# Last stage of a four-layer convolution block: raw results are added a part later from two buffers of their own, and the loads of strips, h2 and the boxes' x2 are issued a step ahead

## The chip, the cores and the metric

One NeuronCore of a Trainium2 chip runs the whole kernel. The time is that of the device, in microseconds (us); before the change the median of three runs is 4706.14 us (4699.86, 4706.14 and 4724.04).

The engines in this text: PE is TensorE (matrix products and transposes), DVE is VectorE, ACT is ScalarE, POOL is GpSimd. SP (SyncE) only issues transfers here; its instruction queue is called SPq. Each engine works through its own list in order, and waits at an instruction until what that instruction needs has been signalled.

## What is computed

An image tensor x of 4 x 384 x 64 x 64 in float32 goes through four layers, each `x = x + layer(group_norm(x))`. The change lies in the fourth alone, a 7x7 convolution, one filter for each channel and batch, whose filter depends on the input:

```python
x_avg = x.mean(axis=(2, 3)); x_max = x.max(axis=(2, 3))
x_w = gelu(x_avg @ w_avg.T + b_avg + x_max @ w_max.T + b_max)
xr  = (x_w[:, :, None] * w_mix[None]).reshape(b, c, 7, 7)
Gx  = sqrt(sum(xr * xr, axis=(2, 3)))            # keepdims
Nx  = Gx / (Gx.mean(axis=1) + EPS)
kern = gamma * (xr * Nx) + beta
out = depthwise_conv(x, kern, padding=3)
```

Here `x` is the normalised input, and `out` is added to the un-normalised one. For a channel and batch, `kern` is a factor times `w_mix` plus a constant `beta`. So the result is a sum of three things: the input itself (x2 below); `a_s` times the convolution with `w_mix`, which doesn't depend on the batch (the "raw" result); and `b_s` times the sum over a 7x7 window (the "boxes").

## The kernel before

There are B = 4 batches and NJ = 3 groups j of P = 128 channels; a tile is one (j, b): 128 channels on the partitions, N = 4096 pixels, 2 MB. The last stage is `phase_g`. It works in float32, and these are its parts.

*Strips.* The convolution wants pixels on the partitions. `to_strips` (L2094) makes them for j = 0 from x2 in SBUF at the beginning. `half_strips` makes them for a later j in two halves of 64 channels, each in six pieces: load a piece of x2 from memory (L2034, tag `y`, two buffers), scale it (L2040, ACT, tile `ax`), transpose it (L2044, PE, `strip_m`), and copy it out of PSUM into `z` (L2049 on DVE, L2051 on ACT).

*Convolution.* `conv7(j, c0)` handles a chunk of 8 channels. Of the chunk's weights `wmix` (L2132, loaded by POOL, four buffers, asked for three chunks ahead) DVE or POOL makes band matrices `toep` (L2151), four a chunk; PE multiplies (L2164, `conv_m`; the profile shows two records for each float32 product, so 64 for a chunk). For j < 2 ACT copies the result to `rest_o` (L2174), and ACT's queue stores it to memory as `raw` (L2179). For j = 2 `rest_o` has been loaded (L2143) with what the boxes have left, DVE adds the convolution (L2176), and SP stores the end result (L2181).

*x2 of the seven tiles not made earlier.* `x2_of`: load `wx` (L2068), and in four quarters load `h2` (L2073, tile `g_h`, tag `w7`, three buffers), scale it into PSUM (L2077, ACT, `x_m`), add (L2078, DVE), take sums of squares and the maximum (L1868, ACT, which writes over `g_h`), store x2 (L2082, POOL). Then `factors` computes `a_s` and `b_s`, which need all batches.

*Boxes.* `boxes(j, b)` loads x2 again (L2059, tile `in_x`, three buffers of 2 MB shared with the x2 tiles). In four parts of 16 rows it sums over rows on POOL (L2223, L2225) and DVE (L2227 to L2242), transposes (L2248, PE, `ht_m`), copies (L2250, ACT, `ht`), sums over columns with a banded matrix (L2273, PE, `box_m`), and adds `b_s` times that into `in_x` (L2275, DVE). A part makes two such pieces, so 12 tiles make 96. For j < 2 a part also loads the raw result (L2203, SPq, tile `in_raw`, 0.5 MB), scales it by `a_s` (L2258, ACT) and adds it (L2259, DVE): 32 parts, called p = 0 to 31 below. A finished tile is stored by POOL, to `out` for j < 2 (L2263) and to `rest` for j = 2 (L2265). The order of tiles is j = 2, 0, 1.

Four buffers of 0.5 MB with the tag `rest` serve `rest_o`, `in_raw` and, at the start, two of `to_strips`' pieces in turn.

*Order.* Everything beside the convolution is written as generators, and the loop in `phase_g` draws on them: a piece of strips at the first step of a chunk; steps of x2 while there are any; after that a step of boxes at each of a chunk's five steps, and two at the first step of every second chunk. The source's order isn't the machine's: the framework's scheduler places each instruction in its engine's list by a clock of its own, as soon as it takes operands and buffers to be free there, so the position in the source is a priority, not a place.

Of the kernel before, what the change touches and what calls it, by code (L numbers as in the profile page):

```python
# [13 lines left out]

# [7 lines left out]
F32 = mybir.dt.float32  # L22
AF = mybir.ActivationFunctionType
# [4 lines left out]
N = H * W  # L28
NJ = 3
P = 128  # L30
# [251 lines left out]
class _Builder:  # L282
# [1592 lines left out]
    def phase_g(self):  # L1875
# [8 lines left out]
        with ExitStack() as ctx:  # L1884
# [34 lines left out]

            x2 = [self.x2_of(j, b) for j, b in ((1, 1), (1, 2), (1, 3), (2, 0), (2, 1), (2, 2), (2, 3))]  # L1920
            x2 = self.in_turn(*x2, self.factors())
            boxes = self.in_turn(*(self.boxes(j, b) for j in (2, 0) for b in range(B)))
            boxes1 = self.in_turn(*(self.boxes(1, b) for b in range(B)))
            self.mix_ahead = []
            for n in range(3):
                self.load_mix(n)
            x2_left = True
            for j in range(NJ):
                for half in range(2):
                    strips = self.half_strips(j + half, 1 - half) if 0 < j + half < NJ else iter(())  # L1930
                    for n in range(8):
                        for k, _ in enumerate(self.conv7(j, 64 * half + 8 * n)):
                            if k == 0:
                                next(strips, None)
                            if not x2_left:
                                for _ in range(2 if k == 0 and n % 2 else 1):
                                    next(boxes, None)
                            elif k == 0 or k == 1 and n % 4 < 3:
                                x2_left = next(x2, "none") != "none"
                    for _ in strips:  # L1940
                        pass
                if j == 1:
                    boxes = self.in_turn(boxes, boxes1)
            for _ in boxes:
# [69 lines left out]
    def pair_scales(self, j):  # L2014

        for half in range(2):
            for u in range(2):
                for k, v in enumerate((self.s_s, self.s_b)):
# [3 lines left out]
                    )  # L2022

    def half_strips(self, j, half):

        nc = self.nc
        for pair in range(2):
            for part in range(3):
                y = self.gt_p.tile([P, 11 * P], F32, tag="y", name="ax2", bufs=2)
                lo, hi = (22 * part - 1) * W, (22 * part + 21) * W  # L2030
                inside = slice(max(lo, 0) - lo, min(hi, N) - lo)
                for u in range(2):
                    src = self.scratch["x2"][2 * pair + u][j][64 * half : 64 * half + 64]
                    nc.sync.dma_start(y[64 * u : 64 * u + 64, inside], src[:, max(lo, 0) : min(hi, N)])  # L2034
                if part == 0:
                    nc.gpsimd.memset(y[:, 0:W], 0.0)
                if part == 2:
                    nc.gpsimd.memset(y[:, N - lo :], 0.0)
                s, b = (self.a_pair[:, j, k, half, pair : pair + 1] for k in range(2))
                nc.scalar.activation(y[:, inside], y[:, inside], AF.Identity, bias=b, scale=s)  # L2040
                for i, (k0, n) in enumerate(((0, 4), (4, 4), (8, 3))):
                    m = self.pm("strip_m")
                    for k in range(n):
                        nc.tensor.transpose(m[:, k * P : (k + 1) * P], y[:, (k0 + k) * P : (k0 + k + 1) * P], self.ident)  # L2044
                    mv = m.rearrange("p (k b c) -> p k b c", b=2, c=64)[:, 0:n]
                    at = 1 + 11 * part + k0
                    zv = self.z[:, 64 * half : 64 * half + 64, at : at + n, 2 * pair : 2 * pair + 2]
                    if i == 1:
                        nc.vector.tensor_copy(zv.rearrange("p c k b -> p k b c"), mv)  # L2049
                    else:  # L2050
                        nc.scalar.copy(zv, mv.rearrange("p k b c -> p c k b"))  # L2051
                yield

# [7 lines left out]

    def x2_of(self, j, b):

        nc = self.nc
        at = lambda v: v[:, j, b : b + 1]
        bias = at(self.g0) if j == NJ - 1 else self.zero
        x = self.gx_tile("x2")
        nc.sync.dma_start(x, self.wx[b][:, j])  # L2068
        for q in range(4):
            sl = slice(q * 1024, (q + 1) * 1024)  # L2070

            h = self.gw_p.tile([P, 1024], F32, tag="w7", name="g_h2", bufs=3)
            nc.sync.dma_start(h, self.h2[b][:, j, sl])  # L2073
            for v in range(2):
                m = self.pm("x2_m")
                part = slice(q * 1024 + v * 512, q * 1024 + v * 512 + 512)
                nc.scalar.activation(m, h[:, v * 512 : v * 512 + 512], AF.Identity, bias=bias, scale=at(self.gh))  # L2077
                nc.vector.tensor_add(x[:, part], x[:, part], m)  # L2078

            self.x2_piece(j, b, q, x[:, sl], h)  # L2080
            yield None
        nc.gpsimd.dma_start(self.scratch["x2"][b][j], x)  # L2082
        yield x

    def to_strips(self, j, b, x, first=False):
# [49 lines left out]
    def conv7(self, j, c0):  # L2135
# [47 lines left out]

    def boxes(self, j, b):

        nc = self.nc
        x = self.load_x2(j, b)
        off = lambda k: self.off[:, j, b, k - 6 : k - 5]  # L2190
        pairs_of = lambda t, r, n: t[:, r * W : (r + 2 * n) * W].rearrange("p (k r w) -> p k r w", r=2, w=W)
        above, last = None, None
        for part in range(4):
            r0 = 16 * part
            edge = above
            if part < 3:

                above = self.gt_p.tile([P, 2, W], F32, tag="edge", name="edge", bufs=2)
                nc.gpsimd.tensor_copy(above, pairs_of(x, r0 + 12, 2)[:, :, 1])

            if j < NJ - 1:
                d = self.gt_p.tile([P, 1024], F32, tag="rest", name="in_raw", bufs=4)
                nc.sync.dma_start(  # L2203
# [51 lines left out]
            self.box_sums(j, b, x, 2 * part + 1, ht)  # L2255
            if j < NJ - 1:
                xp = x[:, part * 1024 : (part + 1) * 1024]
                nc.scalar.activation(d, d, AF.Identity, bias=self.g0[:, j, b : b + 1], scale=self.a_s[:, j, b : b + 1])  # L2258
                nc.vector.tensor_add(xp, xp, d)  # L2259
            if part == 3:  # L2260
                if j < NJ - 1:

                    nc.gpsimd.dma_start(self.out[j].rearrange("(b m) c n -> b (m c n)", b=B)[b].rearrange("(c n) -> c n", c=P), x)  # L2263
                else:
                    nc.gpsimd.dma_start(self.rest[:, :, b], x.rearrange("p (y n) -> p y n", n=P))  # L2265

# [41 lines left out]
```

## Time and profile before

| what | value |
|---|---|
| median of three runs | 4706.14 us |
| profiled execution, device time | 4704.82 us |
| its span in the profile | 4703.1 us |
| granted clock of PE, mean | 0.969 of full |
| last stage, from its first load to the end | 4012.6 to 4703.1 us |

Of the span the busy shares are PE 93%, DVE 61%, ACT 42% and POOL 17%. How to read this: PE's share is an average over the four layers, and the last stage is 690 us of it. A busy PE isn't necessarily at its peak, since matrix products overlap and the profile models their ends. An engine's idle time is put down to whatever came last before the waiting instruction, a "releaser"; `<-DMA` is a transfer that had to land.

The instructions of the stage from 4250 us on that the text comes back to, with their mean durations:

| line, engine | what | number | mean ns |
|---|---|---|---|
| L2164 PE | `conv_m` product | 1764 | 282 |
| L2273 PE | `box_m` product | 768 | 293 |
| L2250 ACT | `ht` copy | 96 | 582 |
| L2258 ACT | scaling of `in_raw` | 32 | 1241 |
| L2259 DVE | adding `in_raw` | 32 | 1558 |
| L2275 DVE | adding a box piece | 96 | 745 |
| L2151 DVE | `toep` | 72 | 1211 |
| L2151 POOL | `toep` | 35 | 2434 |
| L2132 POOL | issuing a `wmix` load | 24 | 591 |

An entry like `x8` in the timeline below stands for eight instructions of one kind in a row; the bracket behind it is the time the engine waited before, and for what.

### The profile page before, as it was taken

Reading aid. Unit: us, or ns where it says so; the run is one execution under the profiler, and the core shown is the slowest. Engines: PE = TensorE matmul, PEld = TensorE weight load, DVE = VectorE, ACT = ScalarE, POOL = GpSimd, SP = SyncE. Lnnn points to the kernel's source line nnn. Section 1 sums busy time; section 2 is a strip of 40 time slices with the busy share of each in tenths; the row PEclk is TensorE's granted clock in tenths of the full one; section 3 lists DMA queues with packets and bytes.
Section 4 is the critical chain, followed back from the end, with each engine's and each line's share of the span. In section 5 each row is a group of like instructions: output and inputs, shape, how many; then the busy total and the mean of one; then the engine's idle time right before and its main releaser. Section 6 shows DMA issues by size and latency. Waiting matters only on the chain. (4 is left out here: it accounts for less than half of the span.)

```text
span 4703.1 us, 49799 instructions
## 1 busy us (share of the span) xinstructions
PE 4354.0 (93%) x18445; PEld 2417.9 (51%) x18445; DVE 2851.5 (61%) x4680; ACT 1992.2 (42%) x2937; POOL 801.9 (17%) x760
## 2 busy tenths in 40 slices
PE   7999999999999999998988999699999999788887
PEld 2233444344443444444548888344444444688887
DVE  7766566655566446545877888655531115777788
ACT  4444444444444444444535666311134334663332
POOL 1000000000000000000025566000000000346554
PEclk9999999999999999998989999799999999898999
DMA  4301211121111111112338999766664336795786
GB/s 145 108 33 52 89 66 68 47 75 41 54 67 65 61 34 67 55 53 82 125 105 284 324 336 327 277 259 255 247 241 173 124 131 228 282 331 173 238 282 211
DMA packets 284321, 730.36 MB, mean 155 GB/s; under 512 B 22331, under 2 KB 122790, under 8 KB 272806
## 3 DMA queue, kind: packets, MB, share of 16 engines
q1 hardware_dynamic: 213096, 407.56, 27.1%
q0 software_dynamic: 38880, 173.96, 9.8%
q10 hardware_dynamic: 32094, 145.57, 7.8%
q8 instruction: 149, 2.44, 0.2%
q14 instruction: 102, 0.84, 0.1%
HBM read 433.13 MB, written 293.86 MB: 155 GB/s over the span
## 5 line engine op out<-in xcount | busy, mean ns | idle before, releaser
L822 ACT ACTIVATE probs<-sc_s 128x1024 f32<-128x1024 f32 x512 | 496.7, 1020 | 687.3 <-PE av L932 588.1
L932 PE MATMUL av<-probs,vt 128*128 128x512 f32 x1536 | 714.8, 602 | 0.0
L1137 DVE SCALAR_TENSOR_TENSOR acc<-band,vecs,acc 128x512 f32<-128x512 f32 x708 | 496.1, 745 | 44.8 <-POOL band L1096 39.6
L1424 PE MATMUL conv_m<-toep,z 128*128 128x192 f32 (+1 forms) x2304 | 447.9, 352 | 21.4 <-DVE z L1353 12.0
L932 PEld LDWEIGHTS av<-probs,vt 128*128 128x128 f32 x1536 | 275.6, 191 | 338.1 <-issue 334.3
L1791 PE MATMUL h_m<-f_h,cm_w_t 128*128 128x512 f32 x1008 | 437.6, 597 | 9.8 <-ACT f_h L1728 7.4
L1424 PEld LDWEIGHTS conv_m<-toep,z 128*128 128x128 f32 x2304 | 403.8, 195 | 45.4 <-ACT d_o L1435 15.3
L2164 PE MATMUL conv_m<-toep,z 128*128 128x128 f32 x3072 | 385.3, 283 | 14.9 <-DVE toep L2151 11.7
L2164 PEld LDWEIGHTS conv_m<-toep,z 128*128 128x128 f32 x3072 | 371.7, 199 | 17.0 <-DVE toep L2151 11.3
L1670 PE MATMUL h_s<-e_tok,cm_w_t 128*128 128x512 f32 x768 | 362.6, 594 | 4.1 <-DVE e_tok L1655 4.1
L1791 PEld LDWEIGHTS h_m<-f_h,cm_w_t 128*128 128x128 f32 x1008 | 192.8, 191 | 254.1 <-issue 239.9
L814 PE MATMUL sc_s<-q,k 32*128 32x512 f32 x2048 | 306.9, 643 | 14.6 <-ACT probs L822 14.4
L1405 POOL TENSOR_TENSOR toep<-w,band 128x1280 f32<-128x1280 f32 x96 | 278.2, 2898 | 201.0 <-PE conv_m L1424 189.0
L1058 PE MATMUL t_m<-w_in_t,xb 128*128 128x384 f32 x768 | 278.4, 497 | 4.1 <-DVE coef L1075 4.0
L968 PE MATMUL proj_m<-xm,w_proj_t 128*128 128x512 f32 x576 | 271.9, 611 | 6.0 <-DVE xm L907 4.9
L1677 ACT COPY e_h<-h_s 128x1024 f32<-128x1024 f32 x96 | 97.2, 1013 | 399.4 <-PE h_s L1670 399.4
L1679 DVE BATCH_NORM_STATS2 h_st<-e_h 128x6 f32<-128x512 f32 x192 | 123.5, 685 | 217.3 <-ACT e_h L1677 217.2
L1670 PEld LDWEIGHTS h_s<-e_tok,cm_w_t 128*128 128x128 f32 x768 | 146.3, 191 | 187.9 <-issue 183.2
L975 DVE SCALAR_TENSOR_TENSOR x_res<-proj_m,bn_c,x_res 128x512 f32<-128x512 f32 x96 | 71.7, 747 | 237.3 <-PE proj_m L968 237.1
L1058 PEld LDWEIGHTS t_m<-w_in_t,xb 128*128 128x128 f32 x768 | 142.7, 192 | 141.2 <-issue 59.1
L1670 PE MATMUL h_s<-z,cm_w_t 128*128 128x512 f32 x384 | 196.1, 592 | 0.0
L837 PE MATMUL av<-probs,vt 128*32 128x512 f32 x1536 | 189.0, 604 | 4.4 <-DVE av_t L866 4.4
(464 smaller groups left out, 6333.2 us busy)
## 6 DMA issues: line engine op xcount, KB each, us to landing
d<-d_o ACTq DMA_DIRECT2D x48, 1024.0 KB
c_d<-d SPq DMA_DIRECT2D x48, 1024.0 KB
hid<-e_h ACTq DMA_DIRECT2D x16, 3072.0 KB
f_h<-hid SPq DMA_DIRECT2D x14, 3072.0 KB
x_in<-in_x SPq DMA_DIRECT2D x96, 256.0 KB
x_res<-in_x SPq DMA_DIRECT2D x32, 768.0 KB
xa<-x_res POOLq DMA_DIRECT2D x32, 768.0 KB, 3.7
xa_out<-xa SPq DMA_DIRECT2D x32, 768.0 KB
```

Source lines behind the costliest of these rows:

```text
L814: nc.tensor.matmul(s[:, g], lhsT=k4[32 * g : 32 * g + 32, c], rhs=q[i][32 * g : 32 * g + 32], start=True, stop=True,)
L822: nc.scalar.activation(p[:, h * 1024 : (h + 1) * 1024], s[:, 2 * h : 2 * h + 2].rearrange("p a b -> p (a b)"), AF.Exp, scale=0.25,)
L837: nc.tensor.matmul(av[k][quarter(g)], lhsT=vt[:, 4 * c + v, quarter(s)], rhs=p[:, v * 512 : (v + 1) * 512], start=c == 0 and not before, s ...
L932: nc.tensor.matmul(av[0], lhsT=vt[:, 4 * c + v, :], rhs=p[:, v * 512 : (v + 1) * 512], start=c == 0 and v == 0, stop=c == 7 and v == 3,)
L968: nc.tensor.matmul(m, lhsT=self.w_proj[:, j, o * P : (o + 1) * P], rhs=xm[:, j], start=j == 0, stop=j == NJ - 1,)
L1058: nc.tensor.matmul(m[:, 0:C], lhsT=xb[:, j], rhs=self.w_in[:, j, :], start=j == 0, stop=j == NJ - 1,)
L1137: nc.vector.scalar_tensor_tensor(out, src(j, k), w, done, ALU.mult, ALU.add)
L1405: eng.tensor_tensor(t, self.w53[:, at : at + 160].rearrange("p (m n) -> p m n", n=8).unsqueeze(2).to_broadcast([P, 20, 8, 8]), band.rearra ...
L1424: nc.tensor.matmul(m[:, c * 256 + to : c * 256 + to + 64 * (k1 - k0)], lhsT=self.z_[:, at : at + P], rhs=t[:, 10 * c + k0 : 10 * c + k1].r ...
L1670: nc.tensor.matmul(s[:, v, :], lhsT=w1[:, j, o * P : (o + 1) * P], rhs=t[j][:, v * 512 : (v + 1) * 512], start=j == 0, stop=j == NJ - 1,)
L1791: nc.tensor.matmul(m, lhsT=w2[:, o, j * P : (j + 1) * P], rhs=h[o][:, v * 512 : (v + 1) * 512], start=o == 0, stop=o == 5,)
L2164: nc.tensor.matmul(m[:, ch % 4 * P : (ch % 4 + 1) * P], lhsT=self.z_[:, at : at + P], rhs=t[:, 8 * c + 2 * i : 8 * c + 2 * i + 2].rearrang ...
```

## The change

*Raw results.* `in_raw` gets a tag of its own, `raw`, with two buffers, and the tag `rest` goes from four to three. Scaling and adding move to `after_part`, which is called at the end of the next part (`due`), so the source has them one part after the load; the store of a tile moves with them. In the changed program these are the load L2248, the add L2220, and the stores L2224 and L2226.

*Strips.* `strip_load` loads piece n + 1 before piece n is scaled and transposed, and one step of the generator goes to the first load alone, so that each piece is worked on a chunk later in the source. The tag `y` keeps two buffers.

*h2.* `x2_rest` runs over the quarters of all seven tiles and loads quarter n + 1, and with a tile's first quarter also its `wx`, before quarter n is used. The tag `w7` keeps three buffers.

*The boxes' x2.* `all_boxes` asks for the next tile's x2 in the fourth step of a tile (of twelve), where before it was asked for at the tile's own first step. The three 2 MB buffers stay.

*wmix.* Three buffers in place of four, and a tile is asked for two chunks ahead.

No arithmetic is added or removed. With the function bodies that only move left out:

```diff
@@ phase_g
-            x2 = [self.x2_of(j, b) for j, b in ((1, 1), (1, 2), (1, 3), (2, 0), (2, 1), (2, 2), (2, 3))]
-            x2 = self.in_turn(*x2, self.factors())
-            boxes = self.in_turn(*(self.boxes(j, b) for j in (2, 0) for b in range(B)))
-            boxes1 = self.in_turn(*(self.boxes(1, b) for b in range(B)))
+            x2 = self.x2_rest((1, 1), (1, 2), (1, 3), (2, 0), (2, 1), (2, 2), (2, 3))
+            x2 = self.in_turn(x2, self.factors())
+            boxes = self.all_boxes([(j, b) for j in (2, 0, 1) for b in range(B)])
+            self.ready_raw = [False] * NJ
             self.mix_ahead = []
-            for n in range(3):
+            for n in range(2):
                 self.load_mix(n)
...
-                if j == 1:
-                    boxes = self.in_turn(boxes, boxes1)
+                self.ready_raw[j] = True
...
+    def strip_load(self, j, half, pair, part):
...
+        y = self.gt_p.tile([P, 11 * P], F32, tag="y", name="ax2", bufs=2)
...
+            nc.sync.dma_start(y[64 * u : 64 * u + 64, inside], src[:, max(lo, 0) : min(hi, N)])
...
     def half_strips(self, j, half):
...
+        parts = [(pair, part) for pair in range(2) for part in range(3)]
+        ahead = [self.strip_load(j, half, *parts[0])]
+        yield
+        for n, (pair, part) in enumerate(parts):
+            if n + 1 < len(parts):
+                ahead.append(self.strip_load(j, half, *parts[n + 1]))
+            y, inside = ahead.pop(0)
...
+            yield
...
-    def x2_of(self, j, b):
...
-        x = self.gx_tile("x2")
-        nc.sync.dma_start(x, self.wx[b][:, j])
-        for q in range(4):
-            sl = slice(q * 1024, (q + 1) * 1024)
-
-            h = self.gw_p.tile([P, 1024], F32, tag="w7", name="g_h2", bufs=3)
-            nc.sync.dma_start(h, self.h2[b][:, j, sl])
+    def x2_load(self, j, b, q):
+
+        if q == 0:
+            self.x2_now[j, b] = self.gx_tile("x2")
+            self.nc.sync.dma_start(self.x2_now[j, b], self.wx[b][:, j])
+        h = self.gw_p.tile([P, 1024], F32, tag="w7", name="g_h2", bufs=3)
+        self.nc.sync.dma_start(h, self.h2[b][:, j, q * 1024 : q * 1024 + 1024])
+        return h
+
+    def x2_rest(self, *tiles):
...
+        self.x2_now, parts = {}, [(j, b, q) for j, b in tiles for q in range(4)]
+        ahead = [self.x2_load(*parts[0])]
+        for i, (j, b, q) in enumerate(parts):
+            at = lambda v: v[:, j, b : b + 1]
+            if i + 1 < len(parts):
+                ahead.append(self.x2_load(*parts[i + 1]))
+            h, x = ahead.pop(0), self.x2_now[j, b]
...
@@ to_strips
-            tag, bufs = ("y", 2) if k0 % 16 else ("rest", 4)
+            tag, bufs = ("y", 2) if k0 % 16 else ("rest", 3)
@@ load_mix
-            t = self.gt_p.tile([P, 8 * 64], F32, tag="wmix", name="wmix", bufs=4)
+            t = self.gt_p.tile([P, 8 * 64], F32, tag="wmix", name="wmix", bufs=3)
@@ conv7
-        self.load_mix(16 * j + c0 // 8 + 3)
-        o = self.gt_p.tile([P, 8, P], F32, tag="rest", name="rest_o", bufs=4)
+        self.load_mix(16 * j + c0 // 8 + 2)
+        o = self.gt_p.tile([P, 8, P], F32, tag="rest", name="rest_o", bufs=3)
...
-    def boxes(self, j, b):
...
-        x = self.load_x2(j, b)
+    def all_boxes(self, tiles):
+
+        x, self.due = self.load_x2(*tiles[0]), None
+        for i, (j, b) in enumerate(tiles):
+            ahead = None
+            for n, _ in enumerate(self.boxes(j, b, x)):
+                if n == 3 and i + 1 < len(tiles):
+                    ahead = self.load_x2(*tiles[i + 1])
+                yield
+            x = ahead
+        self.due()
+
+    def after_part(self, j, b, part, x, d):
+
+        nc = self.nc
+        if d is not None:
+            xp = x[:, part * 1024 : (part + 1) * 1024]
+            nc.scalar.activation(d, d, AF.Identity, bias=self.g0[:, j, b : b + 1], scale=self.a_s[:, j, b : b + 1])
+            nc.vector.tensor_add(xp, xp, d)
+        if part == 3:
...
@@ boxes
-                d = self.gt_p.tile([P, 1024], F32, tag="rest", name="in_raw", bufs=4)
+                d = self.gt_p.tile([P, 1024], F32, tag="raw", name="in_raw", bufs=2)
...
             self.box_sums(j, b, x, 2 * part + 1, ht)
-            if j < NJ - 1:
-                xp = x[:, part * 1024 : (part + 1) * 1024]
-                nc.scalar.activation(d, d, AF.Identity, bias=self.g0[:, j, b : b + 1], scale=self.a_s[:, j, b : b + 1])
-                nc.vector.tensor_add(xp, xp, d)
...
+            if self.due:
+                self.due()
+            self.due = partial(self.after_part, j, b, part, x, d)
```

More of the change, by code (lines that the diff above doesn't have):

```diff
@@ L13 @@
 from contextlib import ExitStack, nullcontext
+from functools import partial
 import numpy as np
@@ L2022, in pair_scales @@
                     )
+    def strip_load(self, j, half, pair, part):
+        nc = self.nc
+        y = self.gt_p.tile([P, 11 * P], F32, tag="y", name="ax2", bufs=2)
+        lo, hi = (22 * part - 1) * W, (22 * part + 21) * W
+        inside = slice(max(lo, 0) - lo, min(hi, N) - lo)
+        for u in range(2):
+            src = self.scratch["x2"][2 * pair + u][j][64 * half : 64 * half + 64]
+            nc.sync.dma_start(y[64 * u : 64 * u + 64, inside], src[:, max(lo, 0) : min(hi, N)])
+        if part == 0:
+            nc.gpsimd.memset(y[:, 0:W], 0.0)
+        if part == 2:
+            nc.gpsimd.memset(y[:, N - lo :], 0.0)
+        return y, inside
@@ L2024, in half_strips @@
     def half_strips(self, j, half):
         nc = self.nc
[L2027 to L2052, printed above, removed]
@@ new lines, in half_strips @@
+        parts = [(pair, part) for pair in range(2) for part in range(3)]
[5 more added lines that the diff above has]
+            y, inside = ahead.pop(0)
+            s, b = (self.a_pair[:, j, k, half, pair : pair + 1] for k in range(2))
+            nc.scalar.activation(y[:, inside], y[:, inside], AF.Identity, bias=b, scale=s)
+            for i, (k0, w) in enumerate(((0, 4), (4, 4), (8, 3))):
+                m = self.pm("strip_m")
+                for k in range(w):
+                    nc.tensor.transpose(m[:, k * P : (k + 1) * P], y[:, (k0 + k) * P : (k0 + k + 1) * P], self.ident)
+                mv = m.rearrange("p (k b c) -> p k b c", b=2, c=64)[:, 0:w]
+                at = 1 + 11 * part + k0
+                zv = self.z[:, 64 * half : 64 * half + 64, at : at + w, 2 * pair : 2 * pair + 2]
+                if i == 1:
+                    nc.vector.tensor_copy(zv.rearrange("p c k b -> p k b c"), mv)
+                else:
+                    nc.scalar.copy(zv, mv.rearrange("p k b c -> p c k b"))
+            yield
@@ L2060, in load_x2 @@
         return x
-    def x2_of(self, j, b):
-        nc = self.nc
-        at = lambda v: v[:, j, b : b + 1]
-        bias = at(self.g0) if j == NJ - 1 else self.zero
-        x = self.gx_tile("x2")
-        nc.sync.dma_start(x, self.wx[b][:, j])
-        for q in range(4):
-            sl = slice(q * 1024, (q + 1) * 1024)
-            h = self.gw_p.tile([P, 1024], F32, tag="w7", name="g_h2", bufs=3)
-            nc.sync.dma_start(h, self.h2[b][:, j, sl])
+    def x2_load(self, j, b, q):
[6 more added lines that the diff above has]
+    def x2_rest(self, *tiles):
+        nc = self.nc
+        self.x2_now, parts = {}, [(j, b, q) for j, b in tiles for q in range(4)]
[5 more added lines that the diff above has]
+            h, x = ahead.pop(0), self.x2_now[j, b]
             for v in range(2):
@@ L2076, in x2_of @@
                 part = slice(q * 1024 + v * 512, q * 1024 + v * 512 + 512)
+                bias = at(self.g0) if j == NJ - 1 else self.zero
                 nc.scalar.activation(m, h[:, v * 512 : v * 512 + 512], AF.Identity, bias=bias, scale=at(self.gh))
                 nc.vector.tensor_add(x[:, part], x[:, part], m)
[L2080 to L2083, printed above, removed]
+            self.x2_piece(j, b, q, x[:, q * 1024 : q * 1024 + 1024], h)
+            yield
+            if q == 3:
+                nc.gpsimd.dma_start(self.scratch["x2"][b][j], x)
+                yield
     def to_strips(self, j, b, x, first=False):
@@ L2182, in conv7, with boxes @@
         yield
-    def boxes(self, j, b):
-        nc = self.nc
-        x = self.load_x2(j, b)
+    def all_boxes(self, tiles):
[5 more added lines that the diff above has]
+                    ahead = self.load_x2(*tiles[i + 1])
+                yield
+            x = ahead
+        self.due()
+    def after_part(self, j, b, part, x, d):
+        nc = self.nc
+        if d is not None:
[3 more added lines that the diff above has]
+        if part == 3:
+            if j < NJ - 1:
+                to = self.out[j].rearrange("(b m) c n -> b (m c n)", b=B)[b].rearrange("(c n) -> c n", c=P)
+                nc.gpsimd.dma_start(to, x)
+            else:
+                nc.gpsimd.dma_start(self.rest[:, :, b], x.rearrange("p (y n) -> p y n", n=P))
+    def boxes(self, j, b, x):
+        nc = self.nc
+        assert j == NJ - 1 or self.ready_raw[j]
         off = lambda k: self.off[:, j, b, k - 6 : k - 5]
@@ L2199, in boxes @@
                 nc.gpsimd.tensor_copy(above, pairs_of(x, r0 + 12, 2)[:, :, 1])
+            d = None
             if j < NJ - 1:
-                d = self.gt_p.tile([P, 1024], F32, tag="rest", name="in_raw", bufs=4)
+                d = self.gt_p.tile([P, 1024], F32, tag="raw", name="in_raw", bufs=2)
                 nc.sync.dma_start(
@@ L2255, in boxes @@
             self.box_sums(j, b, x, 2 * part + 1, ht)
-            if j < NJ - 1:
-                xp = x[:, part * 1024 : (part + 1) * 1024]
[L2258 to L2265, printed above, removed]
+            if self.due:
+                self.due()
+            self.due = partial(self.after_part, j, b, part, x, d)
     def box_sums(self, j, b, x, n, ht):
```

## The prediction

> **What bounds the kernel now.** First I read the page's head and its 40 slices: TensorE (PE) busy 93% of 4703.1 us, a fall at slice 34, where the DMA digits rise. The change touches only the last stage, which starts when `mean<-in_consts` is issued at 4012.6 us, so at most 690 us are in question. Next, the stretches of that stage, cut where its own steps change: x2 tiles until 4250, boxes of j=2 until 4412, then boxes of j=0 and 1, beside the convolution of j=2 from about 4430.
>
> ```profile
> core 0: us, PE busy (x) PEld busy (x) DVE busy (x) ACT busy (x) POOL busy (x), PEclk, DMA share, GB/s
> 4050.00:4250.00 200.00, 171.30 (x1431) 168.65 (x1432) 144.12 (x156) 119.76 (x183) 79.90 (x64) 0.93 0.95 328
> 4250.00:4412.00 162.00, 143.80 (x1170) 140.90 (x1169) 118.96 (x166) 56.89 (x93) 109.41 (x111) 0.93 0.59 184
> 4412.00:4560.00 148.00, 121.91 (x997) 119.67 (x996) 115.28 (x149) 53.89 (x74) 85.31 (x78) 0.91 0.85 261
> 4560.00:4694.00 134.00, 113.13 (x941) 108.00 (x939) 117.72 (x153) 38.84 (x55) 67.64 (x64) 0.99 0.67 230
> ```
>
> Three limits are seen. Until 4250 the DMA engines are full (0.95). From 4250 PE has holes: 18.2, 26.1 and 20.9 us. In the last stretch VectorE (DVE) is busy 117.72 of 134, 88%. Third, who the waiting engines name, from 4412 to 4560 (PE, then ScalarE, ACT), and for SyncE's queue (SPq) from 4395 to 4700:
>
> ```profile
> PE box_m L2273 <- ACT ht L2250: 17.8, 4, 6.6
> PE ht_m L2248 <- ACT z L2051: 8.3, 1, 8.3
> ...
> ACT in_raw L2258 <- DMA in_raw<-raw: 41.3, 11, 9.0
> ACT ax L2040 <- DMA ax<-x: 4.5, 2, 2.4
> ...
> SPq L2203 <- DMA out<-rest_o: 54.7, 11, 9.1
> SPq L2203 <- DVE in_x L2259: 52.0, 13, 11.3
> ```
>
> (Sum, times, longest.) ACT works in order. Where L2258 stands before its `in_raw` has landed, the `ht` copy behind it is late, and PE's next `box_m` with it. The load itself is late because its buffer is: SPq waits for the add (L2259) or for a store of `rest_o`, which shares the tag. Fourth, one such stall in order of time:
>
> ```profile
> 4505.73 0.33 SPq L2059 DMA_DIRECT2D in_x<-x  x1
> ...
> 4506.16 0.38 SPq L2181 DMA_DIRECT2D out<-rest_o  x1
> ...
> 4507.31 9.95 SPq L2203 DMA_DIRECT2D in_raw<-raw  x2
> ...
> 4518.96 1.24 ACT L2258 ACTIVATE in_raw<-in_raw,g,a_s 128x1024 f32<-128x1024 f32 x1 [9.02 <-DMA in_raw<-raw]
> 4520.10 0.56 ACT L2250 COPY ht<-ht_m 128x512 f32<-128x512 f32 x1
> ...
> 4520.72 2.07 PE L2273 MATMUL box_m<-cols,ht 128*128 128x128 f32 x8 [4.77 <-ACT ht L2250]
> ```
>
> A 2 MB `in_x` load stands just ahead of the raw load, which needs 11.65 us (4507.31 to 4518.96). Loads with no such neighbour need 4.1 to 5 (4659.45 to 4663.88).
>
> **What the Trainium skill says.** "DMA: Bandwidth & Descriptors", section "Anatomy of one DMA", states that DMA engines do not wait on semaphores; the issuing sequencer does, before dispatch. The trace agrees: SPq holds the raw load 52.0 us for L2259, and all that is behind it. So only an earlier free buffer starts a load earlier, not an earlier line. The same page's Specifications give about 358 GB/s of HBM for a core; 328 at a share of 0.95 fits. "Perfetto Trace Analysis", section "Optimization Strategy": repeated gaps can mean that there is no buffer for the next tile. That is what `in_raw` shows, at 21 of 32 loads.
>
> **The change, part by part.** Instructions are placed on the engines by a scheduler which goes by its own clock, so I compared the two programs' instruction orders, and counted box pieces (96: each one `ht` copy, one `box_m`, one L2275; 4.4 us a piece, 282 us for the 64 pieces from 4412 to 4694).
>
> *Raw results one part later, in two buffers of their own.* The order of DVE scarcely follows the new place in the source: add p (0 to 31) stands after piece 34+2p before, and after too in 31 of 32 cases. On ACT the scaling of p=0 and 1 goes from `ht` 33 to 2, nine others move later by one or two pieces, one moves earlier by one, the rest stay. Each load p now waits for add p-2 alone. Before, its issue against the end of add p-2 was: at the same time (within 0.3 us) for 11 loads of the 30, later for 7, earlier for 12, because four shared buffers sometimes let it run further ahead. Sum of ACT's waits: where the issue was later it gains (p=6: 2.2 us, 9: 0.8, 12: 0.4, 19: 1.0; p=2 and 3 nothing, as p=2 stands behind the same `in_x` load in both) 4.4 us. Where it was earlier it loses issue time and gets some back by the moved position (p=8: 3.2, 10: 2.1, 13: 0.9, 14: 0.2, 17: 5.1, 25: 1.6) 13.1; p=21 and 23 give back 4.2. Net 13.1-4.4-4.2 = 4.5 us more waiting. PE's waits behind `ht` in 4412 to 4700 are 17.8+13.6 = 31.4 us for 63.5 us of ACT's raw waits, one half, so +2 us. Bounds: -30 (all these waits go) and +26 (below). The stalls of 9.0 and 8.5 us (p=11, 15) stay: the order `in_x`, store, raw load is the same around them.
>
> *The two early raw loads.* p=0 and 1 move from 4395 to a place before the last h2 load, in the stretch where DMA is full. 1.05 MB at 328 GB/s is +3 us, 0 if SPq is waiting there anyway. Their gain at 4412 is nothing: L2258 of p=0 ran there without a wait.
>
> *Strips' pieces.* All strips come one chunk of 8 channels later on PE. The tag `y` keeps two buffers, so the load of piece n still waits for the transposes of n-2, as SPq's 154.3 us on L2034 show. ACT's scaling stands after these transposes by the same distance as before (a quarter chunk in the boxes' stretch; 1.0 chunk on average before, 1.06 after, in the x2 stretch). I take -1 us. Bounds: -14.6 (all that PE waits behind `ht` from 4250 to 4412, where ACT waits 26.0 us for `ax`) and +5 (the longest PE wait on strips, 5.3, once more).
>
> *h2.* Tag `w7` keeps three buffers and SPq already waits 95.7 us for L1868 to free one: loads are three ahead now. PE is idle 28.7 us of these 200, but 0.95 of DMA leaves at most 10 us. I take -3, range -10 to +3.
>
> *Boxes' x2.* These loads already stand a tile ahead on SPq (the first at 4191.9, used at 4262.6), and in the same places after. POOL waited 5.3 us for them in all, off PE's path: 0, range -3 to +2. The stores of boxes on POOL stand at the same box pieces (21, 25, 32, 36, 39, 43), two others within one.
>
> *wmix from four buffers to three, rest from four to three.* A weight tile is asked for two chunks ahead, not three: 2 x 9 us where chunks are fastest (22.3 in 200 us) against a landing of 6.5 us (median) and 11.7 (longest). DVE waited for wmix once, 4.0 us. 0, with +6 as the bound. POOL's DMA issues keep their number. In `to_strips` three buffers of `rest` still cover one batch; 0, +4 at worst. `rest_o` loads gain lead, which nobody missed (L2176 waits only for PE).
>
> No engine gets an instruction more. Sum: +2+3-1-3 = +1, and the chip's reordering noise on top. The profiled execution took 4704.82 (span 4703.1), so 4705.8; it lies 1.3 under the median of 4706.14. Because the unknown bounds reach further down (30+15+10) than up, I set 4705.
>
> **Rivals.** (A) *ACT's raw waits go.* For it: own buffers, and use of the data one part later as the source has it. PE's waits behind `ht` after 4250 are 46.0 us; some 11 of them are the copy's own 0.73 us, so 35 can go. DVE then binds: its idle time is 32.7 us until 4560 and 16.3 after. Some 30 us: 4675. Against it: the positions counted above. (B) *Part of it:* h2 and strips give 6 to 12 us, the raw loads nothing: 4695, still inside what counts as no change. (C) *Slower: the ring of two raw buffers binds.* Load p starts at add p-2, two parts (17.6 us) before add p; into these must go the landing, 1.2 us of scaling and two pieces through ACT, PE and DVE, about 7. It decides as soon as landing exceeds 17.6-8.2 = 9.4 us. Of the loads that start exactly at add p-2 and whose scaling stands two pieces behind, seven waited 0.5, 9.0, 8.5, 0.0, 4.5, 1.7 and 2.2: mean 3.8. For 28 loads that is 105 us, 42 over 63.5 with the one in front; at the share of 0.62 that PE's 39.7 us (with the 8.3) have of 63.5, +26: 4731. Against it: the long ones stand behind `in_x` loads, one in four. (D) *The source moves, the program doesn't:* my forecast.
>
> **Numbers.** Forecast D 0.50, B 0.14, A 0.23, C 0.13. Less than 0.5% (23.5 us) can't be told from no change here. So same 0.64, faster 0.23, slower 0.13. D's own range, 4690 to 4722. To leave no more than two in ten out, it reaches part of the way to A and C: 4679 to 4727.
>
> **What would show it.** Right: ACT's waits for `in_raw` still sum to 50 to 100 us, the longest again 7 to 9 and beside an `in_x` load; `ax` waits after 4250 near 26; DMA share near 0.95 until 4250. Wrong: raw waits under 20 us with DVE over 90% busy from 4412 (A), or waits of 3 us and more at most parts, with SPq held by L2220 (C); a DVE wait for wmix at every chunk would break the sum too.

## The result and the profile after

| kernel | median us | executions | lowest to highest |
|---|---|---|---|
| before | 4707.11 | 20 | 4697.76 to 4724.04 |
| changed | 4695.40 | 20 | 4687.06 to 4708.59 |

The ratio is 0.9976, 95% interval 0.9965 to 0.9987: 11.3 us less (6.1 to 16.5). That is faster beyond doubt, and within the 0.5% that the prediction called no change. The profiled execution of the changed kernel took 4707.54 us (span 4705.8), the second longest of the twenty, at a granted clock of 0.965 where the one of before had 0.969. So the two spans must not be set against each other; waits and orders can.

The stretches of the last stage in the changed kernel, cut at the same times:

```profile
core 0: us, PE busy (x) PEld busy (x) DVE busy (x) ACT busy (x) POOL busy (x), PEclk, DMA share, GB/s
4050.00:4250.00 200.00, 168.14 (x1413) 165.74 (x1413) 141.83 (x153) 116.46 (x179) 79.42 (x61) 0.91 0.94 322
4250.00:4412.00 162.00, 138.99 (x1135) 135.87 (x1134) 121.14 (x160) 58.70 (x95) 108.03 (x111) 0.93 0.58 179
4412.00:4560.00 148.00, 123.60 (x990) 120.86 (x989) 113.92 (x146) 52.67 (x73) 81.29 (x74) 0.90 0.83 260
4560.00:4694.00 134.00, 120.66 (x996) 116.35 (x995) 121.83 (x161) 41.05 (x58) 79.56 (x70) 0.96 0.70 234
```

DMA is as full until 4250 (0.94), and DVE, at 121.83 of 134, is nearer to its limit in the last stretch. PE's holes, in the order of the rows, are 31.9, 23.0, 24.4 and 13.3 us. Next, what PE and then ACT waited for from 4412 to 4560 (sum, times, longest), and what held SyncE's queue before raw loads from 4395 on:

```profile
PE box_m L2311 <- ACT ht L2295: 20.2, 4, 8.2
PE ht_m L2293 <- ACT z L2061: 3.7, 1, 3.7
...
ACT in_raw L2219 <- DMA in_raw<-raw: 24.2, 11, 8.5
ACT ax L2050 <- DMA ax<-x: 15.8, 3, 8.2
```

```profile
SPq L2248 <- DVE in_x L2220: 86.3, 22, 8.9
```

ACT's waits for `in_raw` are still there: 24.2 us here, and 61.2 us over the stage in 25 places, against 63.5 in 21. They are spread more thinly, and of the four long ones of before (8.0, 6.9, 9.0 and 8.5 at the third, 7th, 12th and 16th part) only the first is left, at 8.5; the longest of the others is now 5.8, at the 15th. The stores of `rest_o` no longer hold a raw load (54.7 us before); the add two parts earlier does, with 86.3 us in place of 52.0. In time, at the part where before ACT stood still for 9.02 us:

```profile
4508.93 1.56 SPq L2069 DMA_DIRECT2D in_x<-x  x1
...
4515.93 1.25 DVE L2220 TENSOR_TENSOR in_x<-in_x,in_raw 128x1024 f32<-128x1024 f32 x1 [0.19 <-issue]
...
4517.20 0.37 SPq L2248 DMA_DIRECT2D in_raw<-raw  x1
...
4521.34 0.59 ACT L2295 COPY ht<-ht_m 128x512 f32<-128x512 f32 x1 [1.09 <-PE ht_m L2293]
...
4522.64 1.24 ACT L2219 ACTIVATE in_raw<-in_raw,g,a_s 128x1024 f32<-128x1024 f32 x1 [0.72 <-DMA in_raw<-raw]
4522.87 1.06 PE L2311 MATMUL box_m<-cols,ht 128*128 128x128 f32 x8
```

The 2 MB `in_x` load goes out at 4508.93. The raw load stays back until the add at 4515.93 has ended, 8.3 us behind the big load and no longer 1.6. It then needs 5.4 us to the scaling, not 11.7, and ACT waits 0.72. In the changed kernel 27 of the 30 loads from the third on start within 0.1 us of the end of the add two parts before.

### The profile page after: what moved, and what is told of

Same layout as the page of the kernel before. It is cut to its first block, busy times and chain, and to the rows that moved or that the text cites. A ratio compares the mean times of both kernels' runs of the same rounds, so it can differ in the third digit from the quotient of the medians.

```text
span 4705.8 us, 49802 instructions
## 1 busy us (share of the span) xinstructions
PE 4362.4 (93%) x18445; PEld 2423.8 (52%) x18445; DVE 2859.2 (61%) x4680; ACT 1992.5 (42%) x2937; POOL 807.4 (17%) x760
## 5 line engine op out<-in xcount | busy, mean ns | idle before, releaser
L1138 DVE SCALAR_TENSOR_TENSOR acc<-band,vecs,acc 128x512 f32<-128x512 f32 x708 | 496.2, 746 | 44.8 <-POOL band L1097 39.7
L1425 PE MATMUL conv_m<-toep,z 128*128 128x192 f32 (+1 forms) x2304 | 446.8, 352 | 21.7 <-DVE z L1354 11.9
L1059 PEld LDWEIGHTS t_m<-w_in_t,xb 128*128 128x128 f32 x768 | 143.3, 192 | 141.3 <-issue 60.7
```

The costliest lines, as they stand in the source:

```text
L1059: nc.tensor.matmul(m[:, 0:C], lhsT=xb[:, j], rhs=self.w_in[:, j, :], start=j == 0, stop=j == NJ - 1,)
L1138: nc.vector.scalar_tensor_tensor(out, src(j, k), w, done, ALU.mult, ALU.add)
L1425: nc.tensor.matmul(m[:, c * 256 + to : c * 256 + to + 64 * (k1 - k0)], lhsT=self.z_[:, at : at + P], rhs=t[:, 10 * c + k0 : 10 * c + k1].r ...
```

## The experiments

Each kernel was timed in turns with the kernel before on the same chip, and is compared with the 7 to 52 executions of before from its own series. All differences below are the ratio's, in us of the median of before, with the 95% interval. The other columns come from one traced execution of each kernel. "PE behind `ht`" counts the waits of `box_m`; pieces of strips waited behind the same copies as well, most of all in raw_only (6.0 us), own_bufs (5.9) and before_hold (4.4). "Last stretch" is the time from the first convolution product of j = 2 (before: 4427.8) to PE's last instruction. Medians of times between load, scaling and add are over the parts from the third on.

| kernel | executions | us against before | ACT waits for `in_raw` | PE behind `ht`, from 4412 | last stretch |
|---|---|---|---|---|---|
| before | 20 | 0 | 63.5 | 31.4 | 264.2 |
| changed | 20 | -11.3 (-16.5 to -6.1) | 61.2 | 29.5 | 259.7 |
| raw_only | 14 | -8.0 (-15.5 to 0.0) | 57.9 | 21.7 | 260.7 |
| loads_only | 14 | -3.3 (-9.4 to +2.8) | 63.2 | 39.2 | 264.4 |
| h2_only | 14 | -1.9 (-8.5 to +4.2) | 62.9 | 30.5 | 264.7 |
| strips_only | 22 | -3.3 (-7.5 to +1.4) | 67.8 | 39.7 | 263.5 |
| own_bufs | 14 | -1.4 (-6.6 to +3.8) | 59.9 | 26.2 | 264.4 |
| due_shared | 14 | +3.8 (-1.4 to +8.9) | 78.2 | 33.1 | 271.3 |
| raw3 | 22 | -7.5 (-11.8 to -2.8) | 75.4 | 37.1 | 263.1 |
| split | 14 | -9.4 (-17.0 to -1.9) | 49.4 | 27.5 | 248.8 |
| before_hold | 9 | -21.7 (-29.7 to -13.2) | 8.8 | 13.2 | 244.7 |
| after_hold | 8 | -25.4 (-35.3 to -15.5) | 8.5 | 20.3 | 243.0 |
| after_hold2 | 6 | -27.3 (-37.7 to -16.5) | 8.1 | 7.3 | 250.6 |
| hold_both | 4 | -60.7 (-70.6 to -50.8) | 12.2 | 3.8 | 238.7 |

### Which part of the change it is

Four kernels, each with some parts of the change put back; between them each part is put back at least once. The boxes' x2 and `wmix` have no kernel of their own. The edits:

```diff
# raw_only: strips and h2 loaded where they are used, the boxes' x2 at a
#   tile's own first step, all as before (function bodies left out)
# loads_only: the raw part as before
-    tag="raw", name="in_raw", bufs=2     # rest_o: bufs=3, wmix: bufs=3
+    tag="rest", name="in_raw", bufs=4    # rest_o: bufs=4, wmix: bufs=4
-    self.due = partial(self.after_part, j, b, part, x, d)
+    self.after_part(j, b, part, x, d)
# h2_only, strips_only: loads_only with only that part ahead (bodies left out)
```

raw_only:

> Only the raw part of the change: in_raw in two buffers of its own, scaled and added a part later, rest and wmix down to three buffers; strips, h2 and the boxes' x2 are loaded as before. Theory 1 (the 11.7 us of the change come from earlier h2 and strips, the raw part is worth about nothing): within 4 us of before, ACT's waits for in_raw again 50 to 75 us in sum. Theory 2 (the raw part makes the gain): 8 to 14 us faster than before, and PE's waits behind ht from 4412 us on under 25 us, against 31.4 before.

loads_only:

> The change without its raw part: strips, h2 and the boxes' x2 each loaded a step ahead; in_raw, rest and wmix as before. Theory 1: 8 to 14 us faster than before. Theory 2: within 4 us of before.

h2_only:

> Only h2 a quarter ahead. Theory 1, if h2 carries it: 5 to 10 us faster, and PE's idle time from 4050 to 4250 us down from 28.7 to about 20. If the full DMA engines (share 0.95 there) set the end of that stretch: within 3 us of before.

strips_only:

> Only the strips' pieces a step ahead. Theory 1, if the strips carry it: 5 to 12 us faster, and PE's waits behind ht from 4250 to 4412 us fall from 14.6 to under 6. As the prediction has it (the tag y keeps two buffers, so a load starts no earlier): within 3 us of before, SPq still held some 150 us for strip_m.

The raw part took 8.0 us off, the loads 3.3, together the change's 11.3. The first interval touches zero, the others hold it, and the two overlap widely; by the plain means of the same executions it is 6.9 and 6.8. So the timed runs don't show which share is the larger. What speaks for the raw part is the last stretch: in before, loads_only, h2_only, strips_only and own_bufs it lies between 263.5 and 264.7 us, in raw_only it is 260.7 and in the changed kernel 259.7, each in one execution.

How the loads' share splits isn't settled either, but the traces of all kernels but hold_both, one execution each, fall into two groups twice. From the stage's first h2 load to the 23rd chunk of 8 channels it is 242 to 255 us in the seven kernels with h2 ahead, 257 to 269 in the six without. From the 23rd chunk to the 33rd, the first of j = 2, it is 156 to 169 us in the seven with the strips ahead, 148 to 154 in the six without. This speaks for h2, and for strips ahead giving part of it back. The timed 1.9 us of h2_only (-8.5 to +4.2) and 3.3 of strips_only (-7.5 to +1.4) show neither.

The raw part was then taken apart: the buffers without the moved place, and the moved place without the buffers.

```diff
# own_bufs: raw_only, but
-    self.due = partial(self.after_part, j, b, part, x, d)
+    self.after_part(j, b, part, x, d)
# due_shared: raw_only, but
-    tag="raw", name="in_raw", bufs=2     # rest_o: bufs=3, wmix: bufs=3
+    tag="rest", name="in_raw", bufs=4    # rest_o: bufs=4, wmix: bufs=4
```

own_bufs:

> Of the raw part only the buffers: in_raw in two of its own, rest and wmix down to three, but scaled and added at the end of its own part as before. If the gain of the raw part (8 us in the earlier comparison, PE's waits behind ht from 4412 us on 21.7 against 31.4) comes from separating loads from rest_o's stores: 5 to 8 us faster than before. If it comes from adding a part later: within 3 us of before or slower, PE's waits behind ht 30 or more.

due_shared:

> Of the raw part only the moved place: scaling and adding a part later, with in_raw and rest_o sharing four buffers and wmix four, as before. If the moved place makes the gain: 5 to 8 us faster than before. If the own buffers make it: within 3 us, and SPq again held for stores of rest_o by some 50 us before raw loads.

Neither half alone gains anything that the runs can show, and the moved place with shared buffers has the longest waits for `in_raw` of all (78.2 us), with SPq held 56.3 us for stores of `rest_o` as its second theory had it. Why the two together should give 8 us isn't settled. With the buffers in place, the moved source hardly changes the program: in the traces of own_bufs and raw_only only 4 of ACT's 453 instructions of the stage, and 17 of DVE's 643, stand in another order. Their intervals (-6.6 to +3.8, -15.5 to 0.0) overlap widely, so the two may well be equally fast.

### Is it the ring of two buffers, or the big load in front?

```diff
# raw3: the change, and
-    tag="raw", name="in_raw", bufs=2
+    tag="raw", name="in_raw", bufs=3
-    o = self.gt_p.tile([P, 8, P], F32, tag="rest", name="rest_o", bufs=3)
+    tag, bufs = ("raw", 3) if j < NJ - 1 and c0 % 16 else ("rest", 2)
+    o = self.gt_p.tile([P, 8, P], F32, tag=tag, name="rest_o", bufs=bufs)
# split: the change, and load_x2 without its load; load_quarter loads 1024 of the 4096 columns
+    if n in (3, 5, 7, 9) and i + 1 < len(tiles):
+        self.load_quarter(ahead, *tiles[i + 1], n // 2 - 1)
```

raw3:

> The whole change, but with three buffers for in_raw; rest_o has two, and for j below 2 it takes turns on both tags. If the ring of two raw buffers is what keeps ACT waiting (in the changed kernel 27 of 30 loads start at the very end of the add two parts before): ACT's waits for in_raw fall from 61 to under 25 us, PE's waits behind ht from 29.5 to under 20, and the time lies 5 to 15 us under that of the changed kernel, 16 to 26 under before. If DVE or the transfers bind anyway: waits fall, but the time stays within 4 us of the changed kernel, some 11 us under before.

split:

> The whole change, with each 2 MB x2 load of the boxes cut into four of 0.5 MB, one in each part of the tile before. If a 2 MB load just ahead of a raw load makes the long stalls: issue to scaling of the raw loads beside in_x falls from 8 to 12 us to 5 or 6, the long waits for in_raw (8.5 us) go, and the time lies 3 to 8 us under the changed kernel, 14 to 19 under before. If the stalls come from the buffer alone: no wait changes much, and the time is within 3 us of the changed kernel, some 11 us under before.

The first theory of raw3 fell, and of the second only the time came true: with a third buffer the waits for `in_raw` rose to 75.4 us, and the time stayed within 4 us of the change's. The reason stands in the timeline. One part in the changed kernel (load, scaling, add), then the next-numbered part in raw3:

```profile
4613.18 0.36 SPq L2248 DMA_DIRECT2D in_raw<-raw  x1
...
4617.62 1.24 ACT L2219 ACTIVATE in_raw<-in_raw,g,a_s 128x1024 f32<-128x1024 f32 x1 [2.38 <-DMA in_raw<-raw]
...
4625.91 1.22 DVE L2220 TENSOR_TENSOR in_x<-in_x,in_raw 128x1024 f32<-128x1024 f32 x1
```

```profile
4595.17 0.36 SPq L2249 DMA_DIRECT2D in_raw<-raw  x1
...
4599.66 1.24 ACT L2220 ACTIVATE in_raw<-in_raw,g,a_s 128x1024 f32<-128x1024 f32 x1 [2.42 <-DMA in_raw<-raw]
...
4616.13 1.22 DVE L2221 TENSOR_TENSOR in_x<-in_x,in_raw 128x1024 f32<-128x1024 f32 x1
```

From load to scaling it is 4.44 us in the one and 4.49 in the other, and ACT waits 2.38 and 2.42. What grew is the time that the scaled data lie about until the add: 7.0 us, then 15.2. Over all parts the medians are 5.2 and 5.3 us for the first step, 8.5 and 15.9 for the second. The load started one part earlier, and the scheduler moved the scaling up behind it by the same amount. A deeper ring buys ACT nothing here, since ACT's place in the queue follows the load. The sums for raw3 from 4412 on:

```profile
ACT in_raw L2220 <- DMA in_raw<-raw: 67.1, 21, 8.9
...
PE box_m L2312 <- ACT ht L2296: 37.1, 16, 8.2
```

Splitting the 2 MB loads took the waits for `in_raw` to 49.4 us. The loads beside `in_x` got faster, as the first theory had it: at the third part issue to scaling is 5.7 us in place of 12.1. But ACT's wait there stayed, at 8.3: ACT has stood at its scaling since 4430.32, and the load goes out only at 4432.98, behind a piece of `in_x` for which SPq is held 18.0 us by a store of `rest`. The time is the change's own (-9.4 against -11.3). So the big neighbour does stretch a load, but taking it away bought no time that the runs show. In the trace the last stretch is 10.9 us shorter than the change's and the stage up to there 4 us longer; one execution each doesn't settle that.

### Moving ACT's place

The instruction order shows where the scaling of a part stands among the 96 `ht` copies: before, up to four copies ahead of the part's add, most often two. So it stands ahead of the two copies of its own part, for which PE is waiting, and the scaled data are only added once these are through. `issue_after` queues the instructions of its block on their engine behind a named one, with no wait added.

```diff
# before_hold: the kernel before, and
-                nc.scalar.copy(ht, m)
+                copied = nc.scalar.copy(ht, m)
...
-                nc.scalar.activation(d, d, AF.Identity, ...)
+                with self.tc.issue_after(copied.ins):
+                    nc.scalar.activation(d, d, AF.Identity, ...)
# after_hold: the change, with the same edit
# after_hold2: the change, behind the first ht copy of the next part
```

before_hold:

> The kernel before with one thing more: the scaling of in_raw on ACT is kept behind the second ht copy of its own part, where the scheduler had it one to four copies earlier. Nothing else of the change. If ACT's place for the scaling, and not the buffers, is what makes it wait: ACT's waits for in_raw fall from 63.5 us to under 20, PE's waits behind ht from 4412 us on from 31.4 to under 20, and the time 8 to 20 us under before. If DVE takes the gain back: the waits fall, the time stays within 4 us of before, and DVE waits for in_raw in their place.

after_hold:

> The changed kernel with the scaling kept behind the second ht copy of its own part. If the place is what counts: waits for in_raw from 61 to under 20 us, PE's waits behind ht from 29.5 to under 18, and 8 to 15 us faster than the changed kernel, so 18 to 28 under before. If DVE or the transfers bind: the waits fall, but the time stays 8 to 14 us under before, where the changed kernel is.

after_hold2:

> The changed kernel with the scaling kept behind the first ht copy of the next part, one copy later still, so that the add is later too, by up to one box piece. If the place counts: waits for in_raw under 10 us, and as fast as the milder hold or 2 to 5 us faster. If two buffers then bind, since each load waits for the later add: SPq waits as long as before, ACT's waits for in_raw stay over 15 us, and it is slower than the milder hold.

One held line in the kernel before, with its four shared buffers, its stores of `rest_o` and its 2 MB loads untouched, gives 21.7 us, where the whole change gives 11.3 in its own series (the intervals overlap, -29.7 to -13.2 and -16.5 to -6.1). The gain lies where the line acts: the last stretch goes from 264.2 to 244.7 us, while the stage up to there is 7.6 us longer in this trace.

It isn't the only thing that moved, though. The scheduler placed other instructions anew as well: in before_hold at least 72 of DVE's 646 instructions of the stage and 19 of POOL's 321 stand in another order than before. after_hold is the cleaner test. Against the changed kernel 18 of 643 and 7 of 323 moved, and ACT's waits fell from 61.2 to 8.5, the last stretch from 259.7 to 243.0, and the time from 11.3 under before to 25.4, as its first theory had it; only PE's waits, 20.3, stayed above the 18 expected. ACT's and PE's waits in before_hold from 4412 on, where the first theory is met on both counts:

```profile
ACT ax L2040 <- DMA ax<-x: 16.9, 4, 7.6
ACT in_raw L2259 <- DMA in_raw<-raw: 8.8, 3, 8.1
...
PE box_m L2274 <- ACT ht L2250: 13.2, 12, 5.6
```

What is left of `in_raw` is in the main one wait of 8.1 us at the third part. In time, two parts in a row, each with the second copy of its part and its scaling behind it without a wait:

```profile
4489.02 0.59 ACT L2250 COPY ht<-ht_m 128x512 f32<-128x512 f32 x1 [2.28 <-PE ht_m L2248]
4489.50 1.24 ACT L2259 ACTIVATE in_raw<-in_raw,g,a_s 128x1024 f32<-128x1024 f32 x1
...
4497.06 0.59 ACT L2250 COPY ht<-ht_m 128x512 f32<-128x512 f32 x1
4497.54 1.24 ACT L2259 ACTIVATE in_raw<-in_raw,g,a_s 128x1024 f32<-128x1024 f32 x1
```

The add stands after the same box piece as before in all 32 parts. Nothing was made earlier: from load to scaling it is 11.5 us now, not 5.4, and from the end of the scaling to the add 2.2, not 9.7. Here the slack lies where the load needs it.

With the change beneath it the hold gives 25.4, held one copy later 27.3 (with waits of 8.1, under the 10 expected); the intervals of all three overlap widely, so what the change adds to the hold, and which hold is better, isn't settled.

### The same for the strips

`ax`, the scaling of a strips' piece, waits in the same way: 46.1 us over the stage before, 59.0 in the changed kernel. In the changed kernel's order its 24 places are uneven: two pieces stand behind the 11th `rest_o` copy, the third behind the 20th.

```diff
# hold_both: after_hold2, and
-                            if k == 0:
+                            if k == 1:
                                 next(strips, None)
...
-            nc.scalar.activation(y[:, inside], ...)
+            with self.tc.issue_after(self.act_last.ins):   # ACT's latest rest_o or ht copy
+                nc.scalar.activation(y[:, inside], ...)
```

> The changed kernel with the scaling of in_raw kept behind the first ht copy of the next part, and the strips' scaling (ax) kept behind the copy that ACT has last in the source, one for each chunk of 8 channels. If the scheduler's early place is what makes ACT wait for ax too: ax waits over the stage fall from 59 us in the changed kernel to under 25, and the time lies 5 to 12 us under that of the same kernel without the second hold, 30 to 38 under before. If the full DMA engines set the end of the x2 stretch: the ax waits fall, ACT waits for h2 or PE for the strips in their place, and the time stays about 27 us under before.

The `ax` waits fell as the first theory had it, but the gain is larger than either theory foresaw: 30 to 38 us under before was expected, and it is 60.7 (50.8 to 70.6), 4645.38 us in the median of four executions. It is the fastest kernel of this study, 1.3% under before. ACT's waits for transfers in it, over the stage:

```profile
ACT x_m L2096 <- DMA g_h<-h: 31.7, 8, 6.1
ACT in_raw L2221 <- DMA in_raw<-raw: 12.2, 4, 7.5
...
ACT ax L2051 <- DMA ax<-x: 1.2, 1, 1.2
```

`ax` has 1.2 us left, `h2` about what it had (27.4 before). The two edits of this kernel, the hold and the strips' step at `k == 1`, weren't tried apart, so which of them makes the gain isn't shown. Against after_hold2 the trace gains 9.4 us up to the 23rd chunk, 21.8 from there to the 33rd, where kernels with the strips ahead had lost time (159.6 us in after_hold2, 137.8 here), and 11.9 in the last stretch. The whole stage, from 4012 to PE's last instruction, in the kernel before and then in hold_both (columns as above):

```profile
4012.00:4692.00 680.00, 572.76 (x4666) 555.57 (x4666) 522.36 (x667) 296.80 (x432) 355.88 (x344) 0.93 0.77 255
```

```profile
core 0: us, PE busy (x) PEld busy (x) DVE busy (x) ACT busy (x) POOL busy (x), PEclk, DMA share, GB/s
4012.00:4631.00 619.00, 559.49 (x4666) 542.99 (x4666) 523.49 (x660) 297.09 (x432) 366.82 (x342) 0.96 0.84 280
```

The number of PE records is the same, 4666. Of the 61 us between, 47.7 are idle time of PE (107.2 to 59.5), and 13.3 are PE being busy for less time with the same work. That goes with its mean granted clock, 0.93 and then 0.96, on which more below. From 4412 to 4560 DVE is now busier than PE, 139.56 of 148 us:

```profile
4412.00:4560.00 148.00, 135.83 (x1129) 132.33 (x1128) 139.56 (x178) 59.28 (x81) 98.76 (x92) 0.95 0.93 304
```

## Why the prediction was right, and where it wasn't

*Time.* 4705 was forecast, with 4679 to 4727; it came to 4695.40, or 11.3 us less than before, inside the 0.5% that had a chance of 0.64. That it lies inside is owed to the width of the range, which was drawn to reach towards rivals A and C, and not to the sum: the sum of the parts said +1, and the interval of the gain, 6.1 to 16.5, excludes that. The size is that of rival B. Whether the gain also comes from B's place, strips and h2 with the raw loads at nothing, isn't settled; the last stretch of raw_only speaks against it.

*The raw part, +2.* This is most likely the term that failed: alone it measured -8.0 (-15.5 to 0.0), with the last stretch 3.5 us shorter. The prediction had ACT's waits grow from 63.5 to 68 and took half of that for PE. They came to 57.9 in raw_only and 61.2 in the changed kernel, inside its window of 50 to 100. But "one half" isn't a fixed rate from ACT's waits to PE's: against 31.4 for 63.5 before, loads_only has 39.2 for 63.2, and raw_only 21.7 for 57.9 (27.7 with its strips). It depends on whether PE wants the copy behind the waiting scaling. The step that the stalls of 9.0 and 8.5 us stay, because the order around them is the same, was wrong in itself. They became 0.7 and 1.1 us. At the first of them (the 12th part) the order was the same and the distance wasn't: the raw load went out 8.3 us behind the `in_x` load, not 1.6. At the second (the 16th) it went out nearer, 2.0 us and not 5.2, and needed 10.3 us to the scaling, not 8.5; ACT came to that scaling only 9.2 us after the load had gone out, and so waited little.

Two readings of the traces don't hold as they stand. Beside the first two scalings, not nine but fifteen stand later on ACT in the changed kernel. And loads with no `in_x` load just ahead don't all need 4.1 to 5 us: in the kernel before ACT waited for three such loads that took 5.7, 9.2 and 7.2 us (the 10th, 11th and 19th part).

*What was seen rightly.* That the place of the adds scarcely follows the source, that loads start at the add two parts before, that waits for `in_raw` would stay about as long as they were, that DMA would be as full until 4250 (0.94), and that wmix with three buffers costs nothing (DVE waits 1.7 us for it over the x2 stretch, 4.0 before). The strips (-1) and h2 (-3) lie within their intervals, and so would zero.

*Rival A* priced the removal of ACT's raw waits at some 30 us, with DVE binding next. The price was near: before_hold, which removes 54.7 of the 63.5 us, gave 21.7 (13.2 to 29.7), and after_hold2, with the change beneath it, 27.3. That the change wouldn't remove them was right, too. What the prediction missed is the cure: it looked for it in buffers ("only an earlier free buffer starts a load earlier"), where raw3 shows that an earlier load moves the scaling up as well.

*Rival C*, that the ring of two binds: the loads do start at the add of two parts before, but the waits didn't grow by the 42 us that it had, and a third buffer changed nothing for the better.

*A term that was left out.* The waits of PE were counted at their own length. Long ones also cost clock, as the last section shows; of hold_both's 61 us in the stage, 13.3 are of the kind that goes with it.

## What to carry to other kernels

Where an engine works in order and an instruction on it waits for a transfer while others behind it are wanted at once, look at when its result is used: here it lay unused for 9.7 us after a wait of up to 9.0. Then try moving the consumer back, which costs one line, before adding buffers or issuing loads earlier; with a scheduler that places by its own clock, an earlier load can pull the consumer forward and leave the wait as it was. Afterwards compare the order of the other engines too, since the scheduler may move more than the line that was held. Sum such waits over all the tiles that have the same form: the hold of the second one (`ax`), with waits no longer than the first and together with a moved step of the strips, came with the larger gain.

## What the runs showed of the hardware

*A long stall of PE is followed by a lower clock.* The Trainium skill says on "TensorE: Matmul & The Clock Gate", section "HAM oscillation — how this bites in real kernels", that PE's clock gate goes to half rate when PE is idle for more than about 3.4 us. The trace agrees for long gaps. The stall at 4516 in the kernel before, in five windows of 3.5 us (the third figure from the right is the granted clock):

```profile
4511.00:4514.50 3.50, 3.50 (x34) 3.50 (x33) 3.50 (x5) 0.00 (x0) 2.46 (x2) 1.00 0.92 302
4514.50:4518.00 3.50, 1.45 (x13) 1.26 (x12) 2.45 (x4) 0.00 (x0) 1.49 (x3) 1.00 0.78 256
4518.00:4521.50 3.50, 0.78 (x3) 0.78 (x4) 0.00 (x0) 2.10 (x3) 1.14 (x1) 0.57 0.99 265
4521.50:4525.00 3.50, 3.50 (x19) 3.50 (x18) 2.17 (x4) 1.68 (x3) 1.10 (x2) 0.50 0.53 186
4525.00:4528.50 3.50, 3.50 (x30) 3.29 (x30) 2.20 (x4) 0.73 (x2) 1.50 (x1) 0.96 0.56 150
```

PE runs out of work in the second window, and after 4.77 us of waiting comes back in the third at half the clock. In the fourth window it has 19 instructions where the first had 34; a `conv_m` product takes 421 ns there, and 275 in the first window. The clock records of the last stage, up to PE's last instruction, hold 15 intervals at half rate before, 95.6 us together, all of them 3.4, 6.8 or 10.2 us long. In hold_both it is 11 intervals, 52.7 us of them in the stage. An estimate from these figures: 42.9 us less at half rate, at 421 ns a product in place of 275, are worth up to 14.9 us of busy time, next to the 13.3 measured.

In the last stages of all fourteen traces (from 4003 us on), each of the 136 PE gaps of more than 3.4 us was followed by half rate, which set in within 5.4 us of the gap's beginning; of the 17 gaps between 3.0 and 3.4 us, 13 were. The converse doesn't hold: of 222 intervals at half rate, 71 began with no gap of over 3 us beginning in the 8 us before. So half rate also set in without an idle time as long as the skill names; why isn't known.

*The run-to-run spread goes with the clock.* In the 126 executions of the kernel before that go with the experiments, on three chips, the mean clock lies between 0.964 and 0.971 and the time between 4689 and 4737 us. The mean time is 4715.2 us at 0.966 (25 executions), 4709.8 at 0.967 (37), 4705.8 at 0.968 (31) and 4701.0 at 0.969 (11), so about 5 us for each 0.001. The changed kernel is faster at the same clock too: 4697.6 us at 0.968 (6 executions) and 4690.0 at 0.969 (5). A single profiled execution is uncertain by as much as this whole change, unless its clock is read with it.
